# Where the small matmuls stand in a two-layer attention kernel: norm's parts, the 0/1 matmuls and one free slot

## The chip, the cores and the metric

The kernel runs on one core of one Trainium2 chip, in float32 throughout. A core has five engines that each execute their own queue in order and wait for one another through semaphores: TensorE (PE in the profile; its weight loads are PEld), VectorE (DVE), ScalarE (ACT), GpSimd (POOL) and the sync engine (SP), which here only issues DMAs. Matmuls write to PSUM[...]; everything else lives in SBUF or in DRAM. The metric is the time of one execution on the device, in microseconds (us); lower is better.

## The reference, cut to what matters

The input is 8 images of 56 x 56 positions with 384 channels. Two residual layers follow each other; both look at a 3 x 3 neighbourhood.

```
x = x + outlook0(gn(x))     # 12 heads: per position 12 x 9 x 9 logits, softmax over the last 9,
                            # weights mix the 9 neighbours' values into 9 outputs,
                            # which are added back at the 9 neighbours; then Wo
x = x + outlook1(gn(x))     # 6 heads: per position 6 x 9 logits, softmax over 9,
                            # one weighted sum of 9 neighbours' values; then W_proj

def gn(v, G=32, eps=1e-5):  # mean and variance over (H, W, 12 channels) of each image
    g = v.reshape(B, H, W, G, C // G)
    m, s = mean(g, (1, 2, 4)), var(g, (1, 2, 4))
    return (g - m) / sqrt(s + eps)
```

The norm of layer 1 needs the mean and variance of the whole result of layer 0 for an image, so layer 1 can't begin on an image before layer 0 is through with it.

## The kernel before, in words

**Tiling.** Two images form a pair (`NPAIR = 4`), and a column of a pair has R = 112 rows. The kernel goes through columns, 56 to a pair. Layer 0 has one step for each column, and three more at the end for work that lags (`for step in range(NPAIR * W + LAG)`). Of eight columns, seven make a tile of 128 rows each: 112 rows of their own and 16 of the eighth column, which is shared out among them. So in the steps with `step % SB == NTILE` (step 7, 15, ..., 223) **there are no logits to compute**; such a step is short on TensorE, while VectorE, ScalarE and GpSimd still have the softmax work of the step before it to do.

**One step of layer 0.** `attend` makes the logits of a tile in three parts (`pi`), each a group of three matmuls of 288 columns into one of three PSUM banks (`bank<-wa_t,xn` in the profile), and then the values (`bank<-wv_t,xn`). After each part it calls `between(n)`, which puts other work into TensorE's queue:

- n = 0: four transposes of the next pair's input (`turning`, tile `pt`, PSUM tag "t"); `weigh()`, which queues the softmax of the previous column (VectorE sums and inverts, GpSimd multiplies `at<-at,den`) and GpSimd's partial sums `pre` of the column before that; then one job.
- n = 1: the first half of `fold` for the column three steps back, and the statistics of the transposed block on VectorE.
- n = 2: one job.
- n = 3: the second half of the `pre` sums on ScalarE, the second half of `fold` (its DMAs to the table `ztab`), and, where there are no logits, one more job.

`fold` is where the **0/1 matmuls** are: two matmuls with the constant `shift`, a matrix of zeros and ones, move weights by a row (tile `pw`, four records in the trace, PSUM tag "f", one buffer). Around them are two or four small ScalarE copies into `wts`, VectorE memsets and additions that read `pw`, and after these the DMAs that SP issues.

**Jobs.** `Jobs` is a list of (due step, function) in order of arrival; `run(step, n)` executes up to n from its head as long as they are due. A job that isn't due holds back those behind it. In layer 0, every 7 columns form a patch (eight to a pair); `plan` queues for it four contractions of values with weights (`pc<-z,vp`, two PSUM buffers, tag "c", emptied by ScalarE into `yT`) and six projections (`po<-yT,wo_t`, one buffer, tag "o", emptied by VectorE into `x1t`). They are due 4, 5, 6, 6 and 7, 7, 8, 8, 9, 10 steps after the plan, which is made at step 56p + 7px + 11. After the last patch of a pair, `params_part` is queued three times: the norm of layer 1, cut into three parts by `yield` in `norm_params`. Part 0 is two `bn_aggr` on VectorE; part 1 is a matmul with `gmat` (`pgmean`, PSUM tag "t") and four small VectorE operations that end in `part`; part 2 is a second such matmul (`pgvar`), a square root on ScalarE and two VectorE operations. All three are due at the step of the last projection.

**Layer 1.** A step is again one column, seven to a group (patch), 32 groups and one more to finish. Each step runs one job, then `attend` (one group of three matmuls of 438 columns, `bank<-wc_t,xn`; nothing where the column number is divisible by 8), then one job more. So the second job of a step and the first of the next stand next to each other in TensorE's queue. `fetch` queues the jobs of a group, all due at step 3 of a group: eight contractions (b = 0, 1; t = 0 to 3; the last is half as long) and six projections, 14 jobs for the 14 slots of seven steps. The first projection reads what the last contraction's ScalarE copy wrote to `yT`. `move` (with three 0/1 matmuls of its own, `pw<-at,shift`) stands in step 5 between `attend` and the second job; `normed` puts the next group's activations into ScalarE's queue in step 6, ahead of `attend`.

`matmul` and `transpose` are helpers (L128 and L131 in the profile), and `InOrder` wraps the other engines' operations (L143), so most operations have those lines; they are told apart by their tiles.

Of the kernel before, what the change touches and what calls it, by code (L numbers as in the profile page):

```python
# [15 lines left out]
def two_outlook_layers(  # L16
# [42 lines left out]
    SB = 8  # L59
# [24 lines left out]
    PY1, NPY1, SX1, SY1 = 8, 7, PX + 2, 10  # L84
# [80 lines left out]
    for base, sign in ((0, 1), (NPG - 1, -1)):  # L165
        gpsimd.affine_select(
            out=gmat, in_=gmat, compare_op=ALU.is_ge, fill=0.0,
            base=base, pattern=[[-sign * NPG, G], [0, NPG]], channel_multiplier=sign,
# [6 lines left out]
    for k in range(-1, 2):  # L175
# [3 lines left out]
            base=k, pattern=[[-1, R]], channel_multiplier=1,  # L179
# [6 lines left out]
    NTILE = SB - 1  # L186
# [195 lines left out]
    zs = [patch.tile([P, NZ0 + SPARE], F32, name=f"z_{n}", bufs=1) for n in range(2)]  # L382
    gpsimd.memset(zs[1][:, NZ0:], 0.0)
    zs = [z[:, :NZ0].rearrange("p (n e) -> p n e", n=NPY0) for z in zs]
    jobs = Jobs()
    later = []

    def flush():
        while later:
            later.pop(0)()  # L390
# [31 lines left out]
    def layer0(late, pools):  # L422
# [372 lines left out]
        def plan(pair, px, first, second, last):  # L795

            nm = f"0_{pair}_{px}"
            n_tile = 2
            yT = projected(nm)
            if not pair and not px:  # L800
                load_res(0, 0)

            def contracts(t, b, f):
                for n in range(NC):
                    f(t + n)
                waiting.remove((pair, px, b))

            for b in range(IMG):

                def contract(t, b=b, z=zs[b]):  # L810
                    vp = vps[pair, px, b]
                    pc = ps.tile([P, NCH, n_tile, PY0, PX], F32, tag="c", name=f"pc_{nm}_{b}_{t}", bufs=NC)
                    for n in range(n_tile):
                        py = t * n_tile + n
                        zp = z[: SX0 * SY0, py].rearrange("s (y h m) -> s y h m", y=PY0, h=HEADS0)
                        for h in range(HEADS0):
                            i, j = divmod(h, P // D0)
                            matmul(
                                pc[j * D0 : (j + 1) * D0, i, n],
                                vp[: SX0 * SY0, py, h * D0 : (h + 1) * D0],  # L820
                                zp[:, :, h, :],
                                start=True, stop=True,
                            )
                    rows_of = slice(t * n_tile * PY0, (t + 1) * n_tile * PY0)
                    scalar.copy(
                        yT[:, :, :, b, rows_of], pc.rearrange("p i n y m -> p i m (n y)")
                    )

                for due, t in zip((first, second)[b], range(0, NPY0 // n_tile, NC)):
                    waiting.append((pair, px, b))  # L830
                    jobs.add(due, lambda t=t, b=b, f=contract: contracts(t, b, f))
            if pair == NPAIR - 1 and px == NPX - 1:
                jobs.add(second[-1], clear_bands)
            if px == 0:
                st1s[pair] = stat.tile([P, IMG, NCH, 2 * NPX, 6], F32, tag="st1", name=f"st1_{pair}")

            def project_out(half, j):
                lo, hi = HALVES[half]
                n = (hi - lo) * R
                po = ps.tile([P, 4 * R], F32, tag="o", name=f"po_{nm}_{half}_{j}")  # L840
                project_half(po, wo_t, yT, half, j)
                if j == 0:
                    plan.x1t = late_w.tile([P, NCH, 4, R], F32, tag="x1t", name=f"x1t_{nm}_{half}", bufs=2)
                x1t = plan.x1t
                vector.tensor_tensor(
                    x1t[:, j, : hi - lo], po[:, :n].rearrange("p (m r) -> p m r", r=R),
                    xres[pair, px][:, lo:hi, j, :], ALU.add,
                )
                for b in range(IMG):
                    vector.bn_stats(  # L850
                        st1s[pair][:, b, j, 2 * px + half, :],
                        x1t[:, j, : hi - lo, b * H : (b + 1) * H],
                    )
                if j == NCH - 1:
                    later.append(
                        lambda: sync.dma_start(
                            x1s[pair][px, :, :, lo * R : hi * R],
                            x1t.rearrange("p i m r -> p i (m r)")[:, :, :n],
                        )
                    )  # L860
                    if half:
                        del xres[pair, px]
                        following = divmod(pair * NPX + px + 1, NPX)
                        if following[0] < NPAIR:
                            load_res(*following)

            parts = [(half, j) for half in range(2) for j in range(NCH)]
            for due, part in zip(last, parts):
                jobs.add(due, lambda part=part: project_out(*part))
            if px == NPX - 1:  # L870
                def params_part(n):
                    if n == 0:
                        making["1"] = norm_params(st1s.pop(pair), f"1_{pair}", params1, pair)
                    next(making["1"])

                for n in range(3):
                    jobs.add(last[-1], lambda n=n: params_part(n))

        making = {}
        clearing = list(clears())  # L880
# [44 lines left out]
        for step in range(NPAIR * W + LAG):  # L925
            folding = fold(*divmod(step - LAG, W)) if step >= LAG else iter(())
            turning = turned(step)
            summing = []

            def weigh():  # L930

                normal = 1 <= step < NPAIR * W + 1 and (step - 1) % SB < NTILE
                if normal:
                    normalise(*divmod(step - 1, W))
                if normal and step % SB == NTILE:
                    share_out(*divmod(step - 1, W))
                if 2 <= step < NPAIR * W + 2:
                    summing.append(presum(*divmod(step - 2, W)))
                    next(summing[0])
                if normal and step % SB < NTILE:  # L940
                    share_out(*divmod(step - 1, W))
                if normal:
                    keep_v(*divmod(step - 1, W))

            def between(n):

                if n == 0:
                    next(turning, None)
                    weigh()
                    jobs.run(step, 1)  # L950
                elif n == 1:
                    next(folding, None)
                    next(turning, None)
                elif n == 2:
                    jobs.run(step, 1)
                else:
                    for part in summing:
                        next(part)
                    next(folding, None)
                    if step % SB == NTILE:  # L960
                        jobs.run(step, 1)

            if step < NPAIR * W:
                attend(*divmod(step, W), between)
                upkeep(step)
            else:
                for n in range(K + 1):
                    between(n)
            flush()

            for lag, read, b in ((0, fetch_v, 0), (1, fetch_z, 0), (2, fetch_v, 1), (3, fetch_z, 1)):
                pair, c = divmod(step - LAG - PX - lag, W)
                if pair >= 0 and c % PX == 0 and c // PX < NPX:
                    px = c // PX
                    read(pair, px, b)
                    if lag == 1:
                        final = pair == NPAIR - 1 and px - NPX
                        ends = {-3: (8, 9, 9, 10, 10, 11), -2: (6, 7, 7, 8, 8, 9)}.get(
                            final, (7, 7, 8, 8, 9, 10)
                        )  # L980
                        second = (5, 6) if final == -2 else (6, 6)
                        plan(
                            pair, px, (step + 4, step + 5), [step + n for n in second],
                            [step + n for n in ends],
                        )
# [19 lines left out]
    def layer1(pools, base, last_of_layer0, late_w):  # L1005
# [156 lines left out]
        def fetch(g, due):  # L1162
            pair, px = divmod(g, NPX)
            n_tile = 2
# [8 lines left out]
            for b in range(IMG):  # L1173
# [17 lines left out]
                        pc[:, :, : hi - lo].rearrange("p i n y m -> p i m (n y)"),  # L1191
                    )

                for t in range((NPY1 + n_tile - 1) // n_tile):
                    jobs.add(due, lambda t=t, f=contract: f(t))

            def project_out(half, j):
                lo, hi = HALVES[half]
# [18 lines left out]
                if j == NCH - 1:  # L1217
                    for b in range(NQ):
# [4 lines left out]
                            )  # L1223
                        )

            for half in range(2):
                for j in range(NCH):
                    jobs.add(due, lambda half=half, j=j: project_out(half, j))

        NG = NPAIR * NPX  # L1230
        for step in range((NG + 1) * PX):
# [23 lines left out]
            if g and m == moved:  # L1255
                move(done)
            jobs.run(base + step, 1)
            flush()
            store()
            if m == 1 and g + 1 < NG:  # L1260
# [56 lines left out]
```

## Time and profile before

| | us |
|---|---|
| time, median of 3 runs | 3257.78 (3256.2 to 3262.86) |
| time of the profiled execution | 3250.82 |
| its span, first to last instruction | 3249.1 |
| PE busy | 3093.8 |
| DVE busy | 2059.3 |
| POOL busy | 1532.0 |
| ACT busy | 1087.5 |
| layer 0's steps, 80 to 2120: PE busy | 1954.11 of 2040 |
| passage to layer 1, 2120 to 2220: PE busy | 90.42 of 100 |
| layer 1, 2220 to 3170: PE busy | 932.95 of 950 |
| end, 3170 to 3249: PE busy | 63.55 of 79 |

The table is read from below: TensorE is busy nearly all the time in every stretch but the last, so what can be won without less work is the idle time that remains, some 155 us in all. The views that follow are lists in which each row gives a start, a length, the engine, the operation with output and inputs, the number of instructions merged into it, and in brackets the idle time in front of it with the instruction that ended it. A "x6" behind a matmul stands for three matmuls, as every float32 matmul of this kernel leaves two records.

### The profile page before, as it was taken

The numbers are of one execution on the slowest core, as the hardware profiler recorded it, in microseconds if no ns is written. First come the engines' busy times: TensorE is split into PE (matmuls) and PEld (weight loads), VectorE is DVE, ScalarE is ACT, GpSimd is POOL, SyncE is SP. The second block draws the span as 40 slices with busy tenths as digits, with TensorE's granted clock in tenths as the row PEclk, the third lists the DMA queues.
The fourth block names the chain that finished last, engine by engine and source line by source line (L and its number), as shares of the span: only waits on it lengthen the run. The fifth ranks groups of instructions, "written<-read, shape, count | busy, mean of one in ns | idle before, by whom it ended". The sixth has DMA issues, their size and how long they took to land. (4 is left out here: it accounts for less than half of the span.)

```text
span 3249.1 us, 72789 instructions
## 1 busy us (share of the span) xinstructions
PE 3093.8 (95%) x27640; PEld 2102.9 (65%) x27640; DVE 2059.3 (63%) x4942; ACT 1087.5 (33%) x2862; POOL 1532.0 (47%) x2319
## 2 busy tenths in 40 slices
PE   6899999999999999999999999889999999999998
PEld 5567766766777666777766676646555555655555
DVE  5667776677777677777767677634454545455454
ACT  4334443343344334434333333322222222222221
POOL 2655555554555554545554556454334333334330
PEclk8899999999999999999999999999999999999998
DMA  9699888889997898988877888888888988889896
GB/s 300 212 312 308 295 268 279 293 270 295 302 315 252 271 303 277 289 291 298 266 245 258 292 263 267 289 270 232 219 236 224 235 219 229 238 217 237 227 232 145
DMA packets 614033, 850.85 MB, mean 262 GB/s; under 512 B 264830, under 2 KB 490754, under 8 KB 605362
## 3 DMA queue, kind: packets, MB, share of 16 engines
q1 hardware_dynamic: 516514, 711.31, 71.9%
q0 software_dynamic: 63824, 116.90, 11.4%
q10 hardware_dynamic: 33344, 17.98, 2.2%
q8 instruction: 218, 3.57, 0.5%
q14 instruction: 133, 1.09, 0.1%
HBM read 514.86 MB, written 322.17 MB: 258 GB/s over the span
## 5 line engine op out<-in xcount | busy, mean ns | idle before, releaser
L128 PE MATMUL bank<-wa_t,xn 128*128 128x288 f32 x3528 | 974.4, 413 | 6.9 <-ACT xn L143 3.8
L128 PE MATMUL po<-yT,wo_t 128*128 128x448 f32 (+1 forms) x2304 | 822.2, 499 | 29.5 <-ACT yT L143 17.1
L143 POOL TENSOR_TENSOR at<-at,den 128x972 f32<-128x972 f32 x196 | 440.6, 2248 | 846.7 <-DVE den L143 528.6
L128 PEld LDWEIGHTS bank<-wa_t,xn 128*128 128x128 f32 x3528 | 652.1, 192 | 219.8 <-issue 20.9
L128 PEld LDWEIGHTS po<-yT,wo_t 128*128 128x128 f32 x2304 | 432.4, 192 | 323.1 <-issue 188.0
L143 ACT ACTIVATE at<-at 128x972 f32<-128x972 f32 (+1 forms) x228 | 215.3, 944 | 952.8 <-DVE at L143 937.6
L143 DVE TENSOR_REDUCE mx<-bank 128x36 f32<-128x324 f32 x588 | 284.8, 484 | 334.7 <-PE bank L128 332.1
L1094 POOL DMA_DIRECT2D at<-lgt x392 | 204.9, 527 | 618.4 <-DVE lgt L143 602.5
L128 PE MATMUL bank<-wc_t,xn 128*128 128x438 f32 x1176 | 477.5, 542 | 1.5 <-DMA wc_t<-in_wv 1.5
L143 ACT COPY yT<-pc 128x294 f32<-128x294 f32 (+2 forms) x512 | 199.9, 406 | 799.8 <-PE pc L128 785.8
L128 PEld LDWEIGHTS pc<-z,vp 121*32 121x32 f32 (+1 forms) x17664 | 343.3, 121 | 125.6 <-issue 83.8
L128 PE MATMUL bank<-wv_t,xn 128*128 128x384 f32 x1176 | 415.8, 490 | 0.0
L128 PE MATMUL pc<-z,vp 121*32 121x49 f32 (+1 forms) x17664 | 383.4, 219 | 21.3 <-issue 10.5
L143 DVE TENSOR_TENSOR at<-bank,mx 128x324 f32<-128x324 f32 x588 | 291.2, 495 | 106.0 <-POOL pre L143 39.6
L128 PEld LDWEIGHTS bank<-wc_t,xn 128*128 128x128 f32 x1176 | 215.0, 190 | 176.7 <-issue 164.3
L128 PEld LDWEIGHTS bank<-wv_t,xn 128*128 128x128 f32 x1176 | 222.5, 191 | 133.8 <-issue 11.0
L143 POOL DMA_DIRECT2D vtab<-v x476 | 289.6, 612 | 14.6 <-issue 5.5
L143 POOL TENSOR_TENSOR pre<-at,at 112x108 f32<-112x108 f32 (+1 forms) x440 | 224.3, 526 | 62.2 <-DMA at<-at 48.2
L143 DVE TENSOR_TENSOR lgt<-bank,ba_t 128x54 f32<-128x54 f32 x196 | 42.1, 215 | 292.0 <-PE bank L128 289.2
L143 DVE SCALAR_TENSOR_TENSOR wide<-po,bo_t,wide 128x448 f32<-128x448 f32 (+1 forms) x156 | 97.4, 624 | 200.2 <-PE po L128 200.0
L329 POOL DMA_DIRECT2D vtab<-v x392 | 211.7, 544 | 14.4 <-issue 6.5
L143 ACT ACTIVATE wts<-pre,inside 112x48 f32<-112x48 f32 (+4 forms) x672 | 181.0, 358 | 68.1 <-DMA ztab<-wts 33.4
(111 smaller groups left out, 2785.6 us busy)
## 6 DMA issues: line engine op xcount, KB each, us to landing
z<-ztab SPq DMA_DIRECT2D x64, 2352.0 KB
vp<-vtab SPq DMA_DIRECT2D x64, 1536.0 KB
vp<-vtab SPq DMA_DIRECT2D x64, 945.0 KB
xres<-xT SPq DMA_DIRECT2D x32, 1176.0 KB
ztab<-wts SPq DMA_DIRECT2D x336, 110.2 KB
vtab<-v POOLq DMA_DIRECT2D x108, 336.0 KB, 7.0
xin<-xT SPq DMA_DIRECT2D x52, 672.0 KB
xr<-in_x SPq DMA_DIRECT2D x50, 672.0 KB
```

What stands on the lines that cost most here:

```text
L128: tc.keep_in_program_order(nc.tensor.matmul(*args, **kwargs))
L143: return lambda *args, **kwargs: tc.keep_in_program_order(op(*args, **kwargs))
L329: queue.dma_start(bass.AP(table.tensor, table.offset + first, [*([line * step, count] for step, count in rows_of or ((1, rows),)), *([[(R ...
L1094: nc.gpsimd.dma_start(at_of(g_of)[row : row + n, m_of].rearrange("r k h -> r (k h)"), lg[lo : lo + n])
```

## The change

It has three parts.

1. The three parts of layer 1's norm go into a queue of their own, `norms`, and are due one step after another instead of at the same step. In layer 0 at most one of them runs in a step, at n = 2 behind the job; in layer 1 behind the second job of a step. They no longer take a slot of `jobs`.
2. In steps without logits, the first half of `fold` isn't run at n = 1 but at n = 3, behind the third job; its second half follows at once. (In other steps nothing changes: there the first half still runs at n = 1.)
3. In layer 1 an empty job is put between a group's contractions and its projections; so that a group still has 14 jobs, the first two contractions become one job.

```diff
-    jobs = Jobs()
+    jobs, norms = Jobs(), Jobs()
...
                 for n in range(3):
-                    jobs.add(last[-1], lambda n=n: params_part(n))
+                    norms.add(last[-1] + n, lambda n=n: params_part(n))
...
                 elif n == 1:
-                    next(folding, None)
+                    if step % SB != NTILE:
+                        next(folding, None)
                     next(turning, None)
                 elif n == 2:
                     jobs.run(step, 1)
+                    norms.run(step, 1)
                 else:
                     for part in summing:
                         next(part)
-                    next(folding, None)
                     if step % SB == NTILE:
                         jobs.run(step, 1)
+                        next(folding, None)
+                    next(folding, None)
...
-                for t in range((NPY1 + n_tile - 1) // n_tile):
-                    jobs.add(due, lambda t=t, f=contract: f(t))
+                for ts in ((0, 1), (2,), (3,)) if b == 0 else ((0,), (1,), (2,), (3,)):
+                    jobs.add(due, lambda ts=ts, f=contract: [f(t) for t in ts])
...
+            jobs.add(due, lambda: None)
             for half in range(2):
                 for j in range(NCH):
                     jobs.add(due, lambda half=half, j=j: project_out(half, j))
...
             jobs.run(base + step, 1)
+            norms.run(base + step, 1)
             flush()
```

## The prediction, made before the changed kernel ran

> **What bounds the kernel now.** I read the page's busy shares first, then TensorE's list of waits, then the same list by stretch of time, and last the timeline around each kind of wait.
>
> ```profile
> PE 3093.8 (95%) x27640; PEld 2102.9 (65%) x27640; DVE 2059.3 (63%) x4942; ACT 1087.5 (33%) x2862; POOL 1532.0 (47%) x2319
> ```
>
> TensorE sets the time; no part of the change removes a matmul, so only its 155 us of idle time can shrink or grow. What ends it (total, times, longest):
>
> ```profile
> PE pw L128 <- POOL pre L143: 26.9, 13, 3.8
> PE po L128 <- ACT yT L143: 17.1, 33, 1.4
> PE po L128 <- DVE x1t L143: 12.1, 16, 2.0
> PE pgvar L128 <- DVE part L143: 11.4, 3, 4.0
> ...
> PE pgmean L128 <- DVE mv L143: 6.5, 2, 3.4
> ...
> PE pgmean L128 <- ACT xt L143: 6.2, 2, 3.1
> PE pc L128 <- ACT yT L143: 5.7, 10, 0.9
> ```
>
> The change touches all of these but the first. Layer 1 first, one group's passage from contractions to projections:
>
> ```profile
> 2440.85 1.61 PE L128 MATMUL pc<-z,vp 90*64 90x56 f32 x48
> 2442.39 2.47 PE L128 MATMUL bank<-wc_t,xn 128*128 128x438 f32 x6
> 2444.79 0.56 PE L128 MATMUL pc<-z,vp 90*64 90x56 f32 x12
> 2445.75 2.52 PE L128 MATMUL po<-yT,wo_t 128*128 128x448 f32 x6 [0.40 <-ACT yT L143]
> ```
>
> The short last contraction stands directly before the first projection, which waits for its ScalarE copy. Then step 127, the one without logits in which parts 1 and 2 of a norm run (TensorE; VectorE's line last):
>
> ```profile
> 1217.14 0.60 PE L131 MATMUL pt<-ident,xr 112*128 112x112 f32 x4
> 1220.83 0.38 PE L128 MATMUL pgmean<-mv,gmat 128*128 128x2 f32 x2 [3.08 <-ACT xt L143]
> 1221.07 0.86 PE L128 MATMUL pw<-pre,shift 112*112 112x120 f32 x4
> 1225.92 0.59 PE L128 MATMUL pgvar<-part,gmat 128*128 128x2 f32 x2 [3.98 <-DVE part L143]
> 1226.44 2.19 PE L128 MATMUL pc<-z,vp 121*32 121x49 f32 x96
> 1228.56 3.21 PE L128 MATMUL bank<-wa_t,xn 128*128 128x288 f32 x6
> ...
> 1223.25 2.23 DVE L143 TENSOR_TENSOR part<-mv,gmean 128x2 f32<-128x2 f32 x1
> ```
>
> Both norm matmuls stall TensorE, and the matmuls after the stall are slow: 3.21 us for three logit matmuls that take 1.62 to 1.72 elsewhere. Last, a step without logits that has two projections:
>
> ```profile
> 1518.59 2.50 PE L128 MATMUL po<-yT,wo_t 128*128 128x448 f32 x6
> 1520.92 0.57 PE L128 MATMUL pw<-pre,shift 112*112 112x120 f32 x4
> 1522.88 1.96 PE L128 MATMUL po<-yT,wo_t 128*128 128x336 f32 x6 [1.38 <-DVE x1t L143]
> ```
>
> Here the 0/1 matmuls lie inside a gap: the second projection has to wait for VectorE to empty the one "o" buffer in any case.
>
> **What the Trainium skill says.** "TensorE: Matmul & The Clock Gate", What's actually happening: after an idle window of about 3.4 us the array's clock is halved until it has been busy about as long, and the window runs freely. The trace agrees: 3.21 against 1.62 behind the 3.98 us wait; of four 1.36 us waits in layer 1 two are followed by slow projections (3.98 and 4.08 against 2.52). "GPSIMD Engine Reference", 1. Specifications: GpSimd's SBUF interfaces are shared with VectorE, which contends with two SBUF inputs. The line above agrees: `part` took 2.23 us beside GpSimd's `at<-at,den` (1223.23, 2.22 us) and 0.16 where GpSimd was idle. "Perfetto Trace Analysis", Matmuls: independent groups should rotate through PSUM banks so that emptying one overlaps the next; "o" has one buffer in layer 0, so whatever is put between two projections is what rotates there.
>
> **Part 3, the free slot in layer 1.** Removed: the adjacency. The last contraction moves to step 6's first slot, with 2.4 us of logits behind it before the projection. Its copy stands in ScalarE's queue behind `move`'s (ending 1.0 us after 2440.95), so it is through near 2443.1; the projection would start at 2444.5: no wait. The list for 2200 to 3180 has 30 waits, 15.8 us: 26 of 0.40 and four of 1.36. A gap of 0.40 replaces an overlap of 0.07, so 26 x 0.47 = 12.2 us. In the four, step 6 has no logits, so contraction and projection stay adjacent; but the last copy no longer stands behind `normed` (0.3 to 1.1 us each), only behind `move`'s copies: I work out an idle time of 1.1 instead of 1.74 us (with 0.37 before the last contraction), 4 x 0.7 = 2.8, plus half of the 3.0 us of slow matmuls. **Sum 16.5 us**; from below 10 (if the fused first job makes the third contraction wait, 0.4 us in some groups), from above 20. Fusing the first two contractions costs nothing: both "c" buffers are free then, and logits follow. The values' and weights' DMAs aren't needed earlier, since the same work (four contractions, two logit groups) stands before b = 1 as before, and no `pc` in this stretch waits for a DMA.
>
> **Part 1, the norm, layer 0.** Three steps (71, 127, 183) lose both stalls. In step 127 TensorE will do transposes until 1217.7, then the contraction that was third (1.45, until 1219.2; its `z` was requested at 1190.04 and such a load takes 13.55 in the chain), then `pgmean`, which still waits for VectorE and for `xt` until about 1220.8: 1.6 us of idle time instead of 3.1. Then `pw`, the first logits (until 1223.2), transposes that wait about 1 us until `gmean` has left the shared "t" buffer, a contraction, the second logits until 1227. **What is late next is GpSimd**: `pw` of step 128 needs `pre`, which in this trace is ready at 1228.27 and depends on the softmax sums behind `bn_aggr`, not on TensorE. So that `pw` starts at 1228.3 instead of 1235.06. The same for step 71 (710.1 for 716.55) and step 183 (1741.4 for 1747.16): 6.7 + 6.4 + 5.8 = 18.9, less 0.28 x 3 for `pgvar`, which comes in the next step (`part` is 3 us old by then), less about 1 for a slow clock after the 1.6 us waits: **17 us**, between 8 (VectorE's extra 2.2 us in `part` also pushing the logits' sums) and 20. ScalarE's two table loads (1.28 us each) move with the square root and stay hidden.
>
> **Part 1, layer 1.** Pair 3's norm runs in steps 14 to 16. Removed: 3.44 us (`pgmean` behind `bn_aggr`) and 1.77 of slow matmuls after it (4.14 against 2.37); with a step between the parts nothing waits. **5.2 us**, at least 3.4.
>
> **Part 2, the 0/1 matmuls.** In 28 steps the matmuls, two to four ScalarE copies, one to three memsets and one or two VectorE additions move behind the jobs; the table's DMAs keep their place on SP but start 2 to 3 us later, because the ScalarE copies now stand behind a `pre` copy that waits for GpSimd (1.99 us at 1305.44). Queued behind those DMAs on SP are loads needed steps later; `z` of patch 4, requested in such a step, has four steps (36 us). VectorE's additions then end within about 1 us before `pre` or `pw` of the next step can need their buffers. On TensorE nothing changes where one job or none is due. In the 12 steps with two (patches 2, 3, 4), the second job starts when it did, pinned by `x1t` or `yT`, and `pw` comes after it, 0.57 us that were covered. Step 223, with three projections, likewise: 13 x 0.57 = **7.4 us lost**. From below, none (if VectorE's earlier second emptying saves as much later); from above 15, if the late copies also lengthen the 1.3 to 2.6 us waits for `pre` in the steps after.
>
> **Sum**: 16.5 + 17 + 5.2 - 7.4 = 31.3 us. 3250.82 - 31.3 = 3219.5 for the profiled execution; the median stands 0.21% above it, so **3226**.
>
> **Rivals.**
> (a) As above: 3226.
> (b) Half the wins come back: `pw` in steps 72, 128, 184 waits longer behind GpSimd (8 instead of 17), the slot yields 12, and the move costs 11: 12 + 8 + 5.2 - 11 = 14 us, 3244. For it: 13 waits of `pw` for `pre`, nearly all in steps after one without logits, show how close GpSimd runs there. Against: the time of `pre` can be read off and isn't affected.
> (c) Slower: the move. All 28 folds make ScalarE's copies, VectorE's additions and the table's DMAs late, the next step's `pre` (two buffers, one of them read by that fold) must wait, and TensorE with it. It decides from 38.7 / 28 = 1.4 us a step; at 2.0 it costs 56: 3275. For it: GpSimd's partial sums already end TensorE's largest wait. Against: GpSimd's write into that buffer comes only after 1309.49 in the step after 1301, some 2 us after I expect the additions to end.
> (d) The move is free or better and the slot gives all of 20: 3214.
>
> **Numbers.** Chances: (a) 0.62, (b) 0.19, (c) 0.10, (d) 0.09. The range from 3212 to 3247 takes in (b) and (d) and leaves out (c) and the far ends. About 0.2% (6.5 us) is what a measurement of this kernel can tell from no change; (a), (d) and most of (b) lie beyond it: faster 0.84, same 0.06, slower 0.10.
>
> **What would show it.** In layer 1 `po` waits for `yT` fall from 15.8 to 3 to 5 us, in four groups alone; `pgvar` waits vanish, `pgmean` keeps three of about 1.6; `pw` waits for `pre` of 1 to 2 us appear in steps 72, 128 and 184; waits for `x1t` and `pc`'s for `yT` in layer 0 grow by 0.57 where two jobs are due. I'd be wrong if `po` still waited in every group, or if the 28 steps each grew by more than a microsecond.

## The result, and the profile after

The changed kernel takes **3217.36 us** (median of 4, 3211.32 to 3220.78) where the kernel before takes 3257.96: a ratio of 0.9871, with a 95% interval from 0.9851 to 0.9891. So it is 1.3% faster; 3226 had been predicted. The profiled execution has a span of 3209.6 us against 3249.1, that is 39.5 us less; 31.3 had been worked out.

The page's busy shares after:

```profile
PE 3078.3 (96%) x27640; PEld 2099.1 (65%) x27640; DVE 2058.8 (64%) x4942; ACT 1084.6 (34%) x2862; POOL 1531.1 (48%) x2319
```

And TensorE's list of waits after (total, times, longest):

```profile
PE pw L128 <- POOL pre L143: 29.9, 15, 3.7
PE po L128 <- DVE x1t L143: 15.9, 16, 3.1
...
PE pc L128 <- ACT yT L143: 9.7, 11, 2.2
...
PE po L128 <- ACT yT L143: 4.9, 7, 0.9
...
PE pgmean L128 <- ACT xt L143: 3.5, 2, 1.7
PE pgmean L128 <- DVE mv L143: 2.9, 2, 1.7
...
PE pc L128 <- DMA z<-ztab: 2.1, 1, 2.1
...
PE pgvar L128 <- DVE part L143: 0.8, 1, 0.8
```

The number of matmuls is the same. The waits of `po` for `yT` (17.1 to 4.9) and of `pgvar` (11.4 to 0.8) are nearly gone; those of `po` for `x1t` (12.1 to 15.9), of `pc` for `yT` (5.7 to 9.7) and of `pw` for `pre` (26.9 to 29.9) have grown. What the list doesn't say: TensorE's *busy* time fell too, by 15.5 us, though the work is the same. Stretches of matmuls that ran at a slow granted clock count as busy, and so does the start of a stretch that doesn't overlap the end of the one before.

The same passage of a group in layer 1 as before, now with the free slot (timeline of TensorE):

```profile
2425.85 0.82 PE L128 MATMUL pw<-at,shift 112*112 112x126 f32 x6
2426.60 1.26 PE L128 MATMUL pc<-z,vp 90*64 90x56 f32 x36
2427.79 2.47 PE L128 MATMUL bank<-wc_t,xn 128*128 128x438 f32 x6
2430.11 2.42 PE L128 MATMUL po<-yT,wo_t 128*128 128x448 f32 x6
```

No bracket stands behind the projection: it doesn't wait. Step 127, with the norm in it, and the next:

```profile
1214.98 1.45 PE L128 MATMUL pc<-z,vp 121*32 121x49 f32 x96
1218.16 0.39 PE L128 MATMUL pgmean<-mv,gmat 128*128 128x2 f32 x2 [1.73 <-ACT xt L143]
1218.40 1.06 PE L128 MATMUL pw<-pre,shift 112*112 112x120 f32 x4
1219.25 2.94 PE L128 MATMUL bank<-wa_t,xn 128*128 128x288 f32 x6
...
1225.67 0.67 PE L128 MATMUL pw<-pre,shift 112*112 112x120 f32 x4
```

The contraction fills nearly half of the wait of `pgmean`; the rest, 1.73 us, was still followed by a slow stretch: three logit matmuls took 2.94 us, and the granted clock from 1218.16 to 1222.20 was 0.58. Last, the step with two projections:

```profile
1510.80 2.50 PE L128 MATMUL po<-yT,wo_t 128*128 128x448 f32 x6
1515.09 1.96 PE L128 MATMUL po<-yT,wo_t 128*128 128x336 f32 x6 [1.80 <-DVE x1t L143]
1516.89 0.57 PE L128 MATMUL pw<-pre,shift 112*112 112x120 f32 x4
1517.31 0.29 PE L128 MATMUL pgvar<-part,gmat 128*128 128x2 f32 x2
```

The second projection waits 1.80 instead of 1.38 us, and `pw` now comes on top.

The order of matmuls is fixed, so each `pw` is a milestone. Subtracting its start after from its start before gives what had been won until then:

| until | won so far, us | in this stretch | worked out |
|---|---|---|---|
| layer 0, step 222 | 10.7 | 10.7 | 17 - 6.8 = 10.2 |
| second group's `pw` of layer 1 | 6.7 | -4.1 | 5.2 - 0.6 = 4.6 |
| 31st group's `pw` | 34.3 | 27.6 | 16.5 |
| end | 39.5 | 5.2 | 0 |

Layer 0 came out as worked out; the passage to layer 1 and layer 1 itself are both off, by -8.7 and +11.1 us. Three things have to be known to read this table.

- The changed kernel's second profile (from its second run, below) has 8.0, -7.2, 27.6 and 3.3 us in these four stretches. Only layer 1's 27.6 repeats. The run with the slot alone, which changes nothing in layer 0, comes out 5.6 us behind there. So it is luck that layer 0 agrees to half a microsecond.
- The fused job puts one contraction more, about 0.7 us, ahead of the second group's `pw` (132 records of contractions before it instead of 108). That much of the second row's loss comes back in the last row.
- The runs of norm alone and of the 0/1 matmuls alone change nothing at the end, and yet they too are about 3 us shorter there than the profile before (72.6 and 72.8 us against 75.95). So most of the last row's 5.2 us belongs to that one profile.

### The profile page after: what moved, and what is told of

It reads as the page before. It is cut to its first block, busy times and chain, and to the rows that moved or that the text cites. A ratio compares the mean times of both kernels' runs of the same rounds, so it can differ in the third digit from the quotient of the medians.

```text
span 3209.6 us, 72777 instructions
## 1 busy us (share of the span) xinstructions
PE 3078.3 (96%) x27640; PEld 2099.1 (65%) x27640; DVE 2058.8 (64%) x4942; ACT 1084.6 (34%) x2862; POOL 1531.1 (48%) x2319
## 5 line engine op out<-in xcount | busy, mean ns | idle before, releaser
L128 PE MATMUL po<-yT,wo_t 128*128 128x448 f32 (+1 forms) x2304 | 819.7, 498 | 21.2 <-DVE x1t L143 15.9
L128 PE MATMUL pc<-z,vp 121*32 121x49 f32 (+1 forms) x17664 | 373.0, 218 | 22.3 <-issue 10.5
L128 PEld LDWEIGHTS bank<-wv_t,xn 128*128 128x128 f32 x1176 | 223.4, 192 | 134.0 <-issue 12.1
```

Of the source, the lines that this page charges most:

```text
L128: tc.keep_in_program_order(nc.tensor.matmul(*args, **kwargs))
```

## The experiments

**The parts one at a time.** Each run is the kernel before with one part of the change, or the change without one. First the slot and the fused job.

```diff
+                for ts in ((0, 1), (2,), (3,)) if b == 0 else ((0,), (1,), (2,), (3,)):
+                    jobs.add(due, lambda ts=ts, f=contract: [f(t) for t in ts])
...
+            jobs.add(due, lambda: None)
```

> Part 3 alone: layer 1's free slot and the fused first job; norm and 0/1 matmuls as before. Theory (each place on TensorE pays by itself): 0.81 us in each ordinary group of layer 1 as between the two traces, 0.6 to 1.0 in the four groups without logits in step 6, 27 us in all from the third group on, and up to 4 in the last 80 us: 3226 to 3231, with no wait for yT in ordinary groups. Rival (the slot yields only the 0.40 us waits, and the rest of layer 1's gain comes from the other parts or from the clock): 12 us, 3246.

Measured: 3227.02 against 3254.87 (ratio 0.9913, 0.9894 to 0.9932), 28 us less. Every ordinary group is 0.80 to 0.82 us shorter, as in the changed kernel. The theory holds. It was made from the two traces, in which the 0.81 us stood already; what this run adds is that they come from this part alone.

The norm's own queue alone (the `norms` lines of the diff above the prediction):

> Part 1 alone: norm's parts in their own queue, everything else as before. Theory: steps 72, 128 and 184 begin their 0/1 matmuls 6.4, 6.7 and 5.8 us earlier, or up to 0.6 more each since the 0/1 matmuls now lie inside the wait of pgmean; 18 to 19 us less in layer 0; at the start of layer 1 nothing or up to 3 us given back, where the first contraction waits for z. 3240 to 3244. Rival (the norm's parts need the 0/1 matmuls out of their way to win): under 12 us, 3247 or more.

Measured: 3234.87 (0.9944, 0.9924 to 0.9965), 20 us less: at least as much as was expected. So the norm's parts don't need the 0/1 matmuls out of their way.

The 0/1 matmuls alone (its `folding` lines):

> Part 2 alone: in steps without logits the 0/1 matmuls behind the jobs. Theory: 0.4 to 0.6 us lost in each of the twelve steps with two jobs due, as the second job is pinned by another engine, and 1 us at the end of layer 0: 5 to 7 us slower, 3263 to 3265. In the steps with a norm the 0/1 matmuls leave the gap in front of pgvar: up to 0.6 us lost in each of three. Rival (the move is free, later waits absorb it): 3258 within 2. Second rival (late ScalarE copies and table writes lengthen the waits for pre in the 28 steps after): 10 us or more slower.

Measured: 3261.14 (1.0019, 1.0012 to 1.0026), 6.3 us slower. In its trace nine of the twelve steps with two jobs lose 0.41 to 0.44 us each. TensorE's timeline in one of them, step 47, reads

```profile
485.15 2.50 PE L128 MATMUL po<-yT,wo_t 128*128 128x448 f32 x6
489.45 1.96 PE L128 MATMUL po<-yT,wo_t 128*128 128x336 f32 x6 [1.80 <-DVE x1t L143]
491.25 0.57 PE L128 MATMUL pw<-pre,shift 112*112 112x120 f32 x4
491.66 0.29 PE L128 MATMUL pgvar<-part,gmat 128*128 128x2 f32 x2
```

From the first projection's start to the second's there are 4.30 us; before there were 4.29 (482.49 to 486.78) with `pw` inside them. Another engine pins the second projection, and the 0/1 matmuls are paid where they now stand: 0.41 us from their start to what follows. Neither rival holds.

The change without the move of the 0/1 matmuls, and later the changed kernel and this one again on one chip in five rounds:

> Parts 1 and 3 without part 2. Theory (the parts add up, and the move costs): 5 to 8 us faster than the changed kernel, 3210 to 3212. Rival (the move pays for itself once norm's stalls are gone): no faster than the changed kernel, 3217 or more.

> The changed kernel as it is, beside the same without part 2, on one chip. Theory (the 0/1 matmuls behind the jobs cost about 0.4 us in each of twelve steps and more in step 223): 4 to 7 us slower than the run beside it. Rival (once norm's stalls are gone the move is free): within 2 us.

> Parts 1 and 3 without part 2, once more, beside the changed kernel. Theory: 4 to 7 us faster than the changed kernel, ratio near 0.986. Rival: within 2 us of it.

Measured: 3210.79 (0.9868, 0.9844 to 0.9892) in the first run. Side by side, 3217.29 with the move (0.9878, 0.9862 to 0.9895) and 3205.62 without it (0.9844, 0.9828 to 0.9860). The move costs something between a few us and 12; the size is not settled closer than that. It doesn't pay for itself, and no kernel here is clearly faster than **the change without it**.

**What the 0.81 us of a group are.** The contractions unfused, two projections fused in their place, and the free slot kept:

```diff
                 for t in range((NPY1 + n_tile - 1) // n_tile):
                     jobs.add(due, lambda t=t, f=contract: f(t))
...
+            jobs.add(due, lambda: None)
+            parts = [(half, j) for half in range(2) for j in range(NCH)]
+            for js in (*([part] for part in parts[:4]), parts[4:]):
+                jobs.add(due, lambda js=js: [project_out(*part) for part in js])
```

> Parts 1 and 3 without part 2, with layer 1's first two contractions as two jobs again and the last two projections as one job instead (still 14 jobs and the free slot). Measures what the fused job is worth. Theory (the 0.81 us of a group are 0.58 from the gap in front of the projection[...], and 0.23 from one switch less between contractions and logits): 0.55 to 0.65 us a group, 4 to 7 us slower than with the fused job. Rival (all 0.81 come from the gap): the same time. Second rival (two projections in one slot wait for VectorE): 10 us or more slower, with waits for a projection's bank in the list.

Measured: 3218.87 (0.9897, 0.9875 to 0.9920), 8 us more than the 3210.79 with the fused job. An ordinary group is 0.46 to 0.48 us shorter than before, not 0.81. So the slot is worth 0.47, exactly the gap and its lost overlap. In this run's trace logits stand behind the short last contraction, and they start 0.49 us after it, where before the projection started 0.96 us after it:

```profile
2439.20 0.56 PE L128 MATMUL pc<-z,vp 90*64 90x56 f32 x12
2439.69 2.47 PE L128 MATMUL bank<-wc_t,xn 128*128 128x438 f32 x6
```

Fusing two contractions is then worth 0.34. The starts of the stretches account for that: four stretches of contractions take 5.47 us of a group instead of 5.61 in five, and a stretch of logits followed by projections 2.21 instead of 2.40 followed by contractions. The fused projections don't blur this: all six take 11.94 us of a group in either kernel.

**Is it the slot, or the distance?** The change without the move, and without the empty job: the first projection stands in step 6's second slot, behind the logits as before, and the free slot falls to the end of the group.

```diff
-            jobs.add(due, lambda: None)
```

> Parts 1 and 3 without part 2, and without the empty job: 13 jobs a group, so the first projection runs in step 6's second slot, behind that step's logits, and the free slot falls behind the last projection. Theory (what counts is that logits stand between the last contraction and the first projection, not where the free slot lies): 0.81 us in each ordinary group as with the empty job; within 2 us of the kernel with it, 3209 to 3213. Rival (the copy needs the whole slot, or two projections meeting at the step's edge wait for VectorE): 0.4 us a group back, 11 us, 3222.

Measured: **3376.42** (1.0373, 1.0341 to 1.0406), 121 us slower than the kernel before, against both expectations. TensorE's list of waits begins:

```profile
PE pc L128 <- DMA z<-ztab: 108.1, 30, 6.2
```

Thirty groups wait for `z`, and slow matmuls follow. (The waits of `po` for `yT` are as with the empty job: 5.0 us, 7 times.) SP's timeline around one of them reads

```profile
2399.66 3.49 SPq L143 DMA_DIRECT2D out<-ot  x4
2403.19 2.53 SPq L143 DMA_DIRECT2D z<-ztab  x4
```

and its list of waits has

```profile
SPq L143 <- DVE wide L143: 493.6, 26, 21.5
```

SP issued these in the order of the program. With the projections half a step earlier, the third one's stores of `out` come into SP's queue ahead of the next group's loads of `z`, and wait there up to 21.5 us for VectorE. With the empty job the loads go first; in that kernel SP shows

```profile
2427.97 2.85 SPq L143 DMA_DIRECT2D z<-ztab  x4
...
2436.25 6.63 SPq L143 DMA_DIRECT2D out<-ot  x4
```

and the contraction that needs `z` starts at 2441.58, 13.6 us after the issue. In the other run 7.7 us lie between (2403.19 to 2410.88), of which TensorE waits 3.62. So both readings of the slot were incomplete: the logits between contraction and projection take away the wait, and the *place* of the free slot keeps stores behind loads on another engine's queue.

**The passage to layer 1.** The changed kernel's lines there:

```profile
2180.52 0.38 PE L128 MATMUL pgmean<-mv,gmat 128*128 128x2 f32 x2 [1.24 <-DVE mv L143]
2181.74 0.38 PE L128 MATMUL pgvar<-part,gmat 128*128 128x2 f32 x2 [0.84 <-DVE part L143]
2184.20 2.63 PE L128 MATMUL pc<-z,vp 90*64 90x56 f32 x48 [2.07 <-DMA z<-ztab]
2186.76 4.70 PE L128 MATMUL bank<-wc_t,xn 128*128 128x438 f32 x6
```

Step 16 has no logits and no jobs, so parts 1 and 2 of pair 3's norm again stand next to each other; and the first contraction then waits for `z`; from there to 2191.30 the granted clock was 0.52. Before, the contraction didn't wait, since `pgmean` had held TensorE up:

```profile
2190.38 0.38 PE L128 MATMUL pgmean<-mv,gmat 128*128 128x2 f32 x2 [3.44 <-DVE mv L143]
2190.62 4.14 PE L128 MATMUL bank<-wc_t,xn 128*128 128x438 f32 x6
...
2194.81 0.91 PE L128 MATMUL pc<-z,vp 90*64 90x56 f32 x24
```

Two attempts on the change without the move: pair 3's norm three steps later, and with it the first group's softmax and 0/1 matmuls two steps earlier.

```diff
-                    norms.add(last[-1] + n, lambda n=n: params_part(n))
+                    norms.add(last[-1] + n + 3 * (pair == NPAIR - 1), lambda n=n: params_part(n))
```

> Parts 1 and 3 without part 2, pair 3's norm due three steps later, in steps 17 to 19 of layer 1. Theory (the passage to layer 1 hangs on the chain from the first group's 0/1 matmuls over the table's write and the load of z to the first contraction, some 15.7 us, and norm's stalls lie inside it): both pgmean and pgvar stop waiting, the wait for z grows from 2 to about 5 us, and the passage takes as long as before within 1 us. Rival (norm's stalls count by themselves): 2.1 us of waits and 3 us of slow matmuls go, 4 to 5 us faster.

Measured: 3209.23 (0.9864, 0.9845 to 0.9883), as without it. Norm's waits are gone, and `z` takes their place in full:

```profile
2183.84 2.81 PE L128 MATMUL pc<-z,vp 90*64 90x56 f32 x48 [4.17 <-DMA z<-ztab]
```

```diff
-            first, second, moved = (1, 2, 3) if last else (3, 4, 5)
+            first, second, moved = (1, 2, 3) if last or g == 1 else (3, 4, 5)
```

> As the run before, and the first group's softmax and 0/1 matmuls of layer 1 two steps earlier (steps 1, 2, 3 of its group instead of 3, 4, 5), so that z can be loaded earlier. Theory (the chain of the table's write and z's load sets the passage): the wait for z in front of the first contraction goes, and the passage is 5 to 8 us shorter than with the norm late alone; 3203 to 3207. Rival (the passage is set by norm or by the end of layer 0): no faster. Third way: the softmax then waits for the last logits' DMA and stalls VectorE and so TensorE for 3 to 5 us, no net gain.

Measured: 3215.98 (0.9886, 0.9868 to 0.9904), no gain. My theory of the chain was only half right. The table's write (issued at 2164.7) now goes out 13.4 us ahead of the last store of `x1t` (2178.10) instead of 5.1, but on SP `z` stands behind that store, which waits for VectorE, and is issued at 2178.72; and TensorE meets a new wait of 5.46 us, as a copy to `yT` stands behind the early softmax on ScalarE. In the changed kernel and in both of these runs `z` is issued 0.6 us behind that store, so it is the store that ends last. The table's write is close behind: in the next run the second group's `z` is issued 4.7 us after its table's write (2196.87 to 2201.55), so from the 5.1 us above I estimate that moving the store alone would win about 1 us; that was not tried.

If `z` can't come earlier, the wait could be filled: the first group due one step later, with more contractions fused.

```diff
-                for ts in ((0, 1), (2,), (3,)) if b == 0 else ((0,), (1,), (2,), (3,)):
+                for ts in (((0, 1), (2,), (3,)), ((0,), (1,), (2,), (3,)), ((0, 1), (2, 3)), ((0, 1), (2,), (3,)))[b + 2 * (g == 0)]:
...
-                fetch(done - 1, base + step + 3)
+                fetch(done - 1, base + step + 3 + (g == 2))
```

> Parts 1 and 3, pair 3's norm three steps later, and layer 1's first group due one step later with two pairs of contractions more in one job each, so that logits stand where TensorE waited for z. Theory (z can't be there earlier, so the wait must be filled): the 4.2 us wait for z and its slow matmuls go, 4 to 7 us faster than without: 3203 to 3206. Rival (something behind it is late next, such as yT or the values' load): within 2 us of 3209.

Measured: 3208.69 (0.9854, 0.9839 to 0.9869), no gain that can be told. The wait for `z` shrinks to 1.67 us, and a wait of 2.40 us for the values (`vp<-vtab`, issued behind `z`) appears in the next job: the rival holds.

**Norm away from the short steps.** As the last run, with `norms.add(last[-1] + 2 + n, ...)`, so that no part of a norm runs in or right before a step without logits:

> As the run before, with all of norm's parts due two steps later than in the change, so that in layer 0 none of them runs in a step without logits, nor bn_aggr right before one. Theory (in steps 71, 127, 183 bn_aggr delays the softmax sums by 1.6 us and so pre, for which TensorE waits in the next step): pgmean, gmean and pgvar stop no matmul, pw in steps 72, 128, 184 waits 1.3 to 2.6 us as after any such step; 1.5 to 3 us in each of three, 4 to 8 us faster than the run before: 3197 to 3201. Rival (bn_aggr's 2.8 us on VectorE stall the logits' banks in a step with logits instead): no faster than the run before.

Measured: 3210.36 (0.9860, 0.9845 to 0.9875), no faster. No matmul of the norm in layer 0 waits any more, but

```profile
710.93 0.66 PE L128 MATMUL pw<-pre,shift 112*112 112x120 f32 x4 [2.16 <-POOL pre L143]
711.43 3.06 PE L128 MATMUL bank<-wa_t,xn 128*128 128x288 f32 x6
```

`pw` of steps 72, 128 and 184 waits 2.16, 2.17 and 2.14 us for GpSimd's `pre`, as after other such steps. Behind the first and the third of these waits a slow stretch follows (3.06 and 2.88 us for three logit matmuls), behind the second none (1.63). Against the run of the change without the move, step 72's `pw` comes 0.69 us earlier after the one before it, and the slow stretch takes 1.56 back. The rival's stall of the logits' banks by VectorE isn't there; GpSimd and then the clock set these steps.

## Why the prediction was right, point by point

- **The norm in layer 0.** `pw` of steps 72, 128 and 184 was to come 6.4, 6.7 and 5.8 us earlier; between the two traces it comes 6.2, 6.7 and 5.6 us earlier against the `pw` of the step before it. `pgmean` was to keep three waits of about 1.6: they are 1.72, 1.73 and 1.67. The waits for GpSimd's `pre` were forecast for all three; they show in steps 72 (0.75) and 184 (2.49 us), and in step 128, after the slow stretch, there is none. The run with the norm apart, where all three wait, confirms that GpSimd is late next.
- **The 0/1 matmuls.** The mechanism was right and the size nearly so: 0.41 to 0.44 in place of 0.57 us a step, since 0.57 is their length and 0.41 the distance to what follows. The run of the move alone gave 6.3 us (3.9 to 8.5 from the interval) where 7.4 was put down. Step 223, with three projections, isn't settled: it lost 1.57 us in the first profile and 0.02 in the second, as the projection behind the 3.1 us wait for `x1t` took 4.09 us in one and 2.52 in the other.
- **The free slot in layer 1** was mis-sized: 16.5 us predicted, 27.6 measured. The term that is missing stands behind "Fusing the first two contractions costs nothing": it costs nothing and *gains* 0.34 us a group, one switch of matmul kinds less. The 0.47 a group beside it was right, as the unfused run shows. The four groups without logits in step 6 gave 7.4 us in all for 4.3.
- **The norm in layer 1** failed: "with a step between the parts nothing waits", +5.2 us. With norm alone, 0.4 us were lost from the first group's `pw` of layer 1 to the second's; with the slot alone 1.7, 0.7 of it the contraction that comes earlier; in the changed kernel 3.2. The step between has no logits, and the stall that was removed had been covering the load of `z`. That contractions wait for no DMA had been read from the list for 2200 to 3180, which leaves out the first group's.
- **The end** was put at nothing and gave 5.2 us. Before, the last contractions waited 2.90 us for `z` and 1.60 for the values; in the changed kernel's first profile neither occurs, but in its second one 4.47 us for the values do. That part of the gain isn't steady, and why it varies stays open.
- **The rivals.** (b) fell: its sum was 14 us, 40 were won, and the norm gave about 18 us at its three steps where it had 8. (d) came near in its sum, 3214, but not for its reasons: the move isn't free, and layer 1 gave 27.6 us where it had 20. (c), that the late copies and table writes of 28 folds cost 2 us each, fell with the run of the move alone: 6.3 us in all, and in the changed kernel `pw`'s waits for `pre` total 29.9 instead of 26.9 us, two of the 15 in the steps after a norm.

The errors of the passage and of layer 1, -8.7 and +11.1, nearly cancel; the total was closer than its terms.

## What to carry to other kernels

Where one engine is busy 95% of the time, as TensorE is here, ask for each idle gap which engine is late next: read from the trace when *its* result is ready, as was done for `pre`, and do that for the DMAs at the change of a stage too. Count what stands between two kinds of matmul: fewer, longer stretches won nearly as much here as the wait that was aimed at. And before moving a job by half a step, list what it puts into the queue of the engine that issues the loads: stores that waited for their data held up the loads behind them here, and the kernel came out 121 us slower than before.

## What the runs showed of the hardware that had not been expected

- A switch from logit matmuls to the small contractions and back cost about 0.34 us a time beyond the matmuls themselves (0.81 less 0.47 us a group), none of it listed as idle.
- Waits of 1.4 to 2.6 us were sometimes followed by a stretch at a slow clock and sometimes not. With the norm apart, three logit matmuls took 3.06 us after a wait of 2.16 (granted clock 0.58), and 1.63 after one of 2.17 at the like place of the next pair (granted clock 1.00). The prediction quotes an idle window of about 3.4 us from "TensorE: Matmul & The Clock Gate", What's actually happening, and says that the trace agrees; for these shorter waits it does not, and the measurement decides.
- In the two profiles of the changed kernel the same wait of 2.16 and 2.15 us, for `pw` of step 120, was followed by 2.65 and 1.63 us for three logit matmuls, and the next `pw` came 10.52 and 8.82 us after it. Differences of this kind make single profiles of one kernel differ by several us.
